# Routing, loading and linear attention in a fused expert-and-attention kernel: three small edits to the order of work

## The chip, the cores and the metric

The kernel runs on one core of a Trainium2 chip. The metric is the device time of one execution in microseconds (us). The core has a matrix engine (TensorE, PE in the profile; its weight loads are PEld), three engines for elementwise work (VectorE or DVE, ScalarE or ACT, GpSimd or POOL), and queues from which DMA transfers are issued (SP's, ScalarE's, GpSimd's). Matrix products go into PSUM banks of 128 x 512 numbers; VectorE and ScalarE read them from there. Each engine works through its own instructions in a fixed order.

## What is computed

All numbers are float32. The input x has shape (4, 512, 256). In short:

```
gate   = rmsnorm(x) @ wg + bias(cond)                 # (4, 512, 8)
w, i   = top 2 of softmax(gate)                       # two of eight experts a token
moe    = sum over the two: w * (relu(relu(x W1 + b1) W2 + b2) W3 + b3)
x      = x + linear_attention(moe)                    # 8 heads, blocks of 32 tokens
x      = x + local_attention_layers(cond_attention(x))  # 16 heads over 512 tokens, then 2 layers
```

In the linear attention each head maps q and k to 128 positive features (elu + 1), and inside a block of 32 tokens

```
num = (qp kp^T masked to the block) v;   z = (qp kp^T masked) 1 + 1e-8;   out = num / z
```

## The kernel before

**Order of work.** Instructions are put on the engines by a list scheduler: it keeps dependencies, takes what is ready in its model in the order of the program, and inserts the waits. `tc.keep_in_program_order(ins)` (used through `pinned(...)` on VectorE and `PE.in_order()` on TensorE) ties an instruction behind the one traced just before it on the same engine. A tile pool hands out `bufs` buffers a tag; a new tile waits until the last reader of the old one is done. `mmt(...)` takes a PSUM bank of the kind "mm" (four in the expert stage and four in linear attention).

**Routing** (L1188 to L1388). TensorE transposes x and forms the gates; four transposes (L1236) bring them back into `pt`. A long chain of small VectorE operations then finds the two best experts of each token (`m`, `eqs`, `rest`, L1254 to L1265), counts with three kinds of products (`ptot` L1286, `ppos` L1288 and L1293, `pcnt` L1292), works out a place for each token, and builds one-hot tiles `ol` and `oh` for the `pmap` products (L1377). `busy(n)` (L1391) issues n products of the identity with xres[0] into a bank that nobody reads; before the change it is defined after the routing and called there with 4, and with 1, 4 and 2 after the experts. `weights()` (L1267) turns the two best gates into the mixing weights `tops`: two subtractions on VectorE, two exponentials on ScalarE, a sum, a reciprocal and a product. In the program it is called at j = 1 of the expert loop (L1495), but the scheduler has moved its work into the routing.

**Experts** (L1488 to L1507). 22 slots of one or two tiles of 128 tokens; each loads its expert's weights on SP, gathers tokens with indirect DMAs, runs three layers with ReLU shared between ScalarE and VectorE (`relu`, L1402 and L1404), and scatters rows to the DRAM tensor `ys`.

**Results** (L1525 to L1544). `results(b)` loads the two expert outputs of batch b from `ys` into tiles g0 and g1 (two buffers each): batch 0 in two halves, k = 0 on SP and k = 1 on ScalarE's queue; every other batch in one load each on SP. `weighted(b, gs)` scales g0 on ScalarE (L1539) and combines on VectorE (L1540) into y[b]. Batches 0 and 1 are loaded at once, then batch 0 is combined; batch 1 is combined in `front(1)`, and `front(b)` loads batch b + 2. `front` also adds a bias to xres[b] on GpSimd (L1561).

**Linear attention** (L1547 to L1700). TensorE's order is written out by hand here. `front(b)` transposes y[b] to yT and forms q, k, v; its copies out of PSUM alternate between ScalarE and VectorE (`evac`, L123 and L125). For each pair of heads `features` forms `pf`, two ScalarE passes `ex` (L1599, L1600) and a VectorE pass `f` (L1602); `scores` forms `psc` and masks it into `sc` (L1612). After each four heads `values(d, g)` forms numerators in the bank `pn` and denominators in the bank `pz`, then

```
nc.scalar.activation(z, pz, AF.Identity, bias=eps8)                              # L1631
nc.vector.reciprocal(z[:, half], z[:, half])                                     # L1636
nc.vector.tensor_tensor(d.aT[:, g, half], pn[:, half], z[:, half], ALU.mult)     # L1637
```

so that `pn` is read last by the product on VectorE. `tail` projects aT and adds to xres. The last batch's pieces run beside `cond_front`, the start of the next attention (`pck`, `pcq`, `fterm` on GpSimd), whose exponentials are `cex` (L420).

Of the kernel before, what the change touches and what calls it, by code (L numbers as in the profile page):

```python
# [15 lines left out]
ALU = mybir.AluOpType  # L16
# [4 lines left out]
NT = S // 128  # L21
# [42 lines left out]
def adaln_attn_ffn_kernel(ctx: ExitStack, tc: tile.TileContext, a: dict, out: bass.AP):  # L64
    nc = tc.nc


    class PE:
        pinned = False
# [36 lines left out]
    def bank(kind, name):  # L106
        return ps_now["pool"].tile([128, 512], F32, tag=kind, name=name, bufs=ps_now[kind])

    def mmt(name):
        return bank("mm", name)  # L110
# [41 lines left out]
    ident = const.tile([128, 128], F32, tag="ident", name="ident")  # L152
    make_identity(nc, ident)
    xres = [const.tile([128, NT, H], F32, tag=f"xres{b}", name=f"xres{b}") for b in range(B)]
# [245 lines left out]
    def cond_stage(W, cp, sp, safe, first=None, v1s=None, before=()):  # L400
# [7 lines left out]
        def attend(fill):  # L408
# [26 lines left out]
            for n in range(len(todo) + 2):  # L435
                if n < len(todo):
                    if n and n % 16 == 0:
                        run(pieces[n // 16 - 1])
                    scores(*todo[n])
                while done:  # L440
                    finish(*done.pop())
                if n < len(todo) and n % 16 != 13:
                    fill(n)
                if 0 < n <= len(todo):
                    values(*todo[n - 1])
# [17 lines left out]
        def attend_safe(d):  # L463
# [39 lines left out]
            for t in range(NT):  # L503
                den = cp.tile([128, CH], F32, tag="cden", name="cden")
                po = None
                for g in range(4):
                    exs = scores(t, g, den)
                    if ahead is not None:
                        values(*ahead)
                    if g == 0:  # L510
                        po = acct("pco")
                    ahead = (t, g, exs, den, po)
            values(*ahead)

        def tail(b, d):
# [628 lines left out]
    with ExitStack() as abc:  # L1144
# [7 lines left out]
        with ExitStack() as moe:  # L1152
# [16 lines left out]
            at, parts = 0, []  # L1169
# [7 lines left out]
            xall = a["x"].rearrange("b s h -> (b s) h")  # L1177

            wgs = xp.tile([128, 2, 32], F32, tag="wgs", name="wgs")
            nc.gpsimd.memset(wgs, 0.0)
# [2 lines left out]
            def pinned(ins):  # L1185
                tc.keep_in_program_order(ins)

            with PE.in_order():  # L1188
# [29 lines left out]
                for c in range(2):  # L1218
                    for b in range(B):
                        PE.matmul(pg[32 * b : 32 * b + 32, :], wgs[:, c, :], xTs[2 * b + c],  # L1220
                                  start=(c == 0), stop=(c == 1))
# [11 lines left out]
            gate = xp.tile(G, F32, tag="gate", name="gate")  # L1233
            pt = tpt("pgt")
            for t in range(NT):
                PE.transpose(pt[:, t * 128 : (t + 1) * 128], gT[:, t * 128 : (t + 1) * 128], ident)  # L1236
            g4 = gate.rearrange("p (b t) e -> p b t e", b=B)
            nc.vector.tensor_tensor(
                g4, pt.rearrange("p (t b e) -> p b t e", b=B, e=32)[:, :, :, 0:NE],
# [6 lines left out]
            def bc(t):  # L1246
                return t.unsqueeze(2).to_broadcast(G)
# [5 lines left out]
            tops = []  # L1253
# [12 lines left out]

            def weights():  # L1267

                nc.vector.tensor_tensor(gate, gate, bc(tops[0]), ALU.subtract)
                nc.scalar.activation(gate, gate, AF.Exp)  # L1270
                nc.vector.tensor_tensor(tops[1], tops[1], tops[0], ALU.subtract)
                nc.scalar.activation(tops[1], tops[1], AF.Exp)
                nc.vector.reduce_sum(tops[0], gate, axis=AX.X)
                nc.vector.reciprocal(tops[0], tops[0])
                nc.vector.tensor_tensor(tops[1], tops[1], tops[0], ALU.mult)
# [15 lines left out]
            pcnt = mmt("pcnt")  # L1291
            PE.matmul(pcnt[:, :NE], tot, mtiles[:, 128:], start=True, stop=True)  # L1292
            PE.matmul(ppos[:, :128], tot, mtiles[:, :128], start=False, stop=True)  # L1293
            E2 = [128, NE, 2 * NE]
            over = xp.tile(E2, F32, tag="over", name="over")
            nc.vector.tensor_tensor(over, pcnt[:, :NE].unsqueeze(2).to_broadcast(E2),
                                    mthr.unsqueeze(1).to_broadcast(E2), ALU.is_gt)

# [60 lines left out]
            for i0 in range(0, B * NT, 4):  # L1359
# [15 lines left out]
                for i in range(i0, i1):  # L1375
                    for k in range(2):
                        PE.matmul(pmap[64 * k : 64 * k + 64, :NHI], ol[:, k, i - i0, :], oh[:, k, i - i0, :],  # L1377
                                  start=(i == 0), stop=(i == B * NT - 1))
# [7 lines left out]
            rowtok = xp.tile([128, NROWT], I32, tag="rowtok", name="rowtok")  # L1386
            nc.vector.tensor_scalar(rowtok, pmap2[:, :NROWT], -1.0, 0.0, ALU.add, ALU.max)
            nc.vector.tensor_single_scalar(rowtok, rowtok, B * S - 1, op=ALU.bitwise_and)  # L1388


            def busy(n):  # L1391
                with PE.in_order():
                    ps = mmt("pbusy")
                    for _ in range(n):
                        PE.matmul(ps, ident, xres[0].rearrange("p t h -> p (t h)")[:, :512], start=True, stop=True)


            busy(4)

            def relu(dst, src, bias):  # L1400
# [87 lines left out]
            for j, d in enumerate(often):  # L1488
                if j == len(often) - 1:
                    aside = conditions(cw_, wp)  # L1490
                    next(aside)
                if j == len(often) - 2:
                    halves = nc.values_load(nhalf[0:1, 0:1], min_val=0, max_val=2 * NE)
                if j == 1:
                    weights()  # L1495
                h1 = layer(d, d.xbT, "h1", d.w1[:, 8:].rearrange("p (c m) -> p c m", m=ME), 0)
                if j:
                    last(j - 1, ds[j - 1])
                if j + 1 < len(often):
                    loads(j + 1, ds[j + 1])  # L1500
                    gather(j + 1, ds[j + 1])
                    if j > 1 and later:
                        name, behind[0] = next(iter(later)), True
                        cw_[name] = later.pop(name)()
                        behind[0] = False
                d.h2 = layer(d, h1, "h2", d.w2, 4)
            last(len(often) - 1, often[-1])  # L1507

            next(aside)
            busy(1)  # L1510
            with tc.If(halves > NHALF - NRARE):
                for j in rare:
                    d = ds[j]
# [4 lines left out]
                    last(j, d)  # L1518
            next(aside)
            busy(4)  # L1520
            run(aside)
            busy(2)


            def results(b):  # L1525
                gs = [gp.tile([128, NT, H], F32, tag=f"g{k}", name=f"g{k}", bufs=2) for k in range(2)]
                n = 2 if b == 0 else NT
                for t in range(0, NT, n):
                    for k in range(2):
                        at = 1 + (k * B + b) * S + t * 128  # L1530
                        queue = nc.scalar if b == 0 and k == 1 else nc.sync
                        queue.dma_start(gs[k][:, t : t + n, :],
                                        ys[at : at + n * 128].rearrange("(t p) h -> p t h", p=128))
                return gs

            def weighted(b, gs):
                for t in range(NT):
                    i = b * NT + t
                    nc.scalar.mul(gs[0][:, t, :], gs[0][:, t, :], tops[0][:, i : i + 1])  # L1539
                    nc.vector.scalar_tensor_tensor(  # L1540
                        y[b][:, t, :], gs[1][:, t, :], tops[1][:, i : i + 1], gs[0][:, t, :], ALU.mult, ALU.add)

            both = {b: results(b) for b in range(2)}
            weighted(0, both[0])  # L1544


        with ExitStack() as lin:  # L1547
# [69 lines left out]
            def values(d, g):  # L1617
                if g == 0:

                    pool, tag = (wp, "aTlast") if d is ds[-1] else (lp, "aT")  # L1620
                    d.aT = pool.tile([128, 2, S], F32, tag=tag, name="aT")
                pn, pz = mmt("pn"), mmt("pz")
                for t in range(NT):
                    for dst in (pn, pz):
                        for i in range(4):
                            h = 4 * g + i
                            lhs = d.v[:, t, 32 * h : 32 * h + 32] if dst is pn else ones32
                            PE.matmul(dst[32 * i : 32 * i + 32, t * 128 : (t + 1) * 128], lhs,
                                      d.scs[h][:, t, :], start=True, stop=True)
                z = lp.tile([128, S], F32, tag="z", name="z", bufs=1)  # L1630
                nc.scalar.activation(z, pz, AF.Identity, bias=eps8)  # L1631

                n = S // 2 if d is ds[-1] and g == 1 else S
                for at in range(0, S, n):
                    half = slice(at, at + n)
                    nc.vector.reciprocal(z[:, half], z[:, half])  # L1636
                    nc.vector.tensor_tensor(d.aT[:, g, half], pn[:, half], z[:, half], ALU.mult)  # L1637

            def tail(b, d):
                for t2 in range(NT // 2):  # L1640
# [30 lines left out]
            with PE.in_order():  # L1671
# [9 lines left out]
                for k in range(len(steps) + 1):  # L1681
                    b, u = steps[k] if k < len(steps) else (B, 0)
# [171 lines left out]
```

## Time and profile before

| | us |
|---|---|
| median of the runs shown (1377.8, 1381.41, 1935.3) | 1381.41 |
| the profiled execution | 1378.49 |
| its span, first to last instruction | 1376.6 |

Busy time of the engines in the stages of the profiled execution (us):

| stage, us from the start | PE | DVE | ACT | POOL | clock granted to PE |
|---|---|---|---|---|---|
| 0 to 20: load, gates | 11.55 | 9.37 | 10.77 | 3.62 | 1.00 |
| 20 to 50: routing, first tokens | 18.32 | 16.05 | 5.89 | 7.71 | 0.77 |
| 200 to 300: experts | 100.00 | 20.64 | 14.93 | 21.54 | 1.00 |
| 300 to 340: results, start of linear attention | 36.62 | 19.36 | 19.29 | 5.41 | 0.96 |
| 340 to 420: linear attention | 75.25 | 57.84 | 47.12 | 0.00 | 1.00 |
| 420 to 500: its end, next attention | 77.28 | 53.61 | 40.21 | 8.37 | 1.00 |

How to read what follows: a row of the timeline gives the start, the time taken, the engine, the line of the kernel, the operation, what it writes and reads, how many instructions are merged, and in brackets how long the engine had been idle and what ended that. A TensorE product in float32 shows as two records. Where several instructions are merged, the time is that from the first start to the last end. A line of a helper (L78 and L82 for products and transposes, L123 and L125 for copies) stands for all its callers, so products are told apart by the tile that they write.

### The profile page before, as it was taken

How to read it: one execution, taken by the hardware profiler on the slowest of the kernel's cores; microseconds unless marked ns; L12 is line 12 of the kernel's file. 1: busy time of each engine (PE TensorE's matmuls, PEld its weight loads, DVE VectorE, ACT ScalarE, POOL GpSimd, SP SyncE). 2: the span in 40 equal slices, each digit the busy share in tenths (PEclk: the TensorE clock that was granted, in tenths of full speed). 3: DMA queues.
4: the chain of work that ended last, by engine and by line, in shares of the span. 5: the costliest groups of instructions: out<-in, count | busy, mean ns of one | idle time of the engine just before them, and what ended most of it. 6: DMA issues, size and time to landing. Idle time of an engine off the chain costs nothing.

```text
span 1376.6 us, 19525 instructions
## 1 busy us (share of the span) xinstructions
PE 1336.3 (97%) x7628; PEld 830.3 (60%) x7628; DVE 653.6 (47%) x1295; ACT 595.8 (43%) x1125; POOL 232.3 (17%) x223
## 2 busy tenths in 40 slices
PE   5999999999999999999999999999999999999998
PEld 4788888884566633433345556656555565556654
DVE  6222121225777743332237697653361777854421
ACT  4111111115555365565656755662222666574111
POOL 1324322211000021010103132000030322310110
PEclk8999999999999999999999999999999999999999
DMA  4577767543000000000220001211001010011000
GB/s 140 208 243 270 238 227 249 192 148 130 1 1 1 1 1 1 1 1 0 89 73 1 18 25 32 86 32 24 24 0 42 24 33 25 17 41 44 20 24 25
DMA packets 43086, 94.74 MB, mean 69 GB/s; under 512 B 9569, under 2 KB 25065, under 8 KB 40169
## 3 DMA queue, kind: packets, MB, share of 16 engines
q1 hardware_dynamic: 37560, 81.81, 18.3%
q0 software_dynamic: 3792, 10.24, 2.3%
q10 hardware_dynamic: 1632, 1.34, 0.3%
q8 instruction: 63, 1.03, 0.3%
q14 instruction: 39, 0.31, 0.1%
HBM read 84.08 MB, written 7.21 MB: 66 GB/s over the span
## 4 chain that ended last, share of the span: by engine, by line
PE 89%; DVE 5%; ACT 2%; DMA 1%; issue 1%; SPq 0%; POOLq 0%; POOL 0%; DVEq 0%
PE ph L78 14%; PE pdq L78 12%; PE pfy L78 6%; PE pug L78 5%; PE sc L78 5%; PE pua L78 5%; PE pv L78 5%; PE po L78 5%; PE pn L78 4%; PE pdy L78 4%; PE pds L78 4%; PE pz L78 2%; PE pqt L82 2%; PE pqk L78 1%; PE pck L78 1%
## 5 line engine op out<-in xcount | busy, mean ns | idle before, releaser
L78 PE MATMUL pdq<-wqkv,yT 128*128 128x512 f32 x384 | 177.1, 603 | 0.2 <-ACT yT L602 0.2
L420 ACT ACTIVATE cex<-sc 128x512 f32<-128x512 f32 x256 | 132.2, 603 | 85.5 <-PE sc L78 85.5
L78 PE MATMUL ph<-h,w 128*128 128x256 f32 (+1 forms) x704 | 132.8, 346 | 1.0 <-issue 1.0
L628 POOL TENSOR_TENSOR qr<-t,t 128x512 f32<-128x512 f32 x64 | 85.9, 1342 | 266.2 <-DVE t L625 225.2
L672 DVE TENSOR_TENSOR p<-p,lmask 128x384 f32<-128x384 f32 (+1 forms) x128 | 92.2, 735 | 69.4 <-ACT p L670 68.2
L78 PEld LDWEIGHTS ph<-h,w 128*128 128x128 f32 x704 | 116.1, 191 | 13.1 <-issue 1.3
L1402 ACT ACTIVATE h<-ph,w 128x256 f32<-128x256 f32 (+1 forms) x88 | 35.4, 438 | 190.7 <-PE ph L78 128.6
L78 PEld LDWEIGHTS pdq<-wqkv,yT 128*128 128x128 f32 x384 | 69.7, 190 | 78.4 <-issue 72.6
L670 ACT ACTIVATE p<-pds,ss 128x256 f32<-128x256 f32 (+1 forms) x256 | 96.1, 457 | 39.1 <-PE pds L78 30.7
L1404 DVE TENSOR_SCALAR h<-ph,w 128x256 f32<-128x256 f32 (+1 forms) x88 | 36.1, 438 | 160.3 <-PE ph L78 102.6
L78 PE MATMUL sc<-qm,kT 32*128 32x512 f32 x512 | 80.6, 639 | 0.0
L78 PE MATMUL pug<-hT,w 128*128 128x512 f32 x160 | 76.8, 602 | 0.0
L618 ACT ACTIVATE sq<-pdq 128x512 f32<-128x512 f32 x64 | 38.3, 598 | 85.4 <-PE pdq L78 47.7
L78 PE MATMUL pua<-hT,w 128*128 128x512 f32 x160 | 75.2, 592 | 0.0
L78 PE MATMUL ph<-xbT,w 128*128 128x256 f32 (+1 forms) x352 | 68.8, 347 | 0.6 <-ACT xbT L123 0.5
L78 PE MATMUL pv<-cex,v 128*32 128x512 f32 x512 | 68.6, 604 | 0.0
L390 POOL TENSOR_SCALAR fterm<-vw,faT 128x256 f32<-128x256 f32 x16 | 14.6, 925 | 316.2 <-DVE cr L380 316.2
L78 PE MATMUL po<-w,h 128*128 128x256 f32 x296 | 67.6, 379 | 0.0
L78 PE MATMUL pds<-qT,kT 64*128 64x256 f32 (+1 forms) x512 | 65.3, 375 | 0.0
L78 PEld LDWEIGHTS pds<-qT,kT 64*128 64x128 f32 x512 | 43.9, 186 | 32.9 <-issue 25.8
L78 PEld LDWEIGHTS ph<-xbT,w 128*128 128x128 f32 x352 | 58.5, 191 | 7.6 <-issue 0.8
L78 PE MATMUL pdy<-wo,oT 128*128 128x256 f32 x256 | 61.5, 386 | 0.0
(301 smaller groups left out, 2130.3 us busy)
## 6 DMA issues: line engine op xcount, KB each, us to landing
w<-in_moe_w_dram SPq DMA_DIRECT2D x22, 1024.0 KB
w<-in_moe_w_dram SPq DMA_DIRECT2D x22, 640.0 KB
w<-in_moe_w_dram SPq DMA_DIRECT2D x22, 516.0 KB
zb<-rows SPq DMA_DIRECT2D x32, 256.0 KB
g<-ys SPq DMA_DIRECT2D x6, 512.0 KB
wqkv<-in_f_wqkv_dram SPq DMA_DIRECT2D x2, 1536.0 KB
w<-in_f_w_dram SPq DMA_DIRECT2D x2, 1408.0 KB
out_dram<-yc SPq DMA_DIRECT2D x16, 128.0 KB
```

Source lines behind the costliest of these rows:

```text
L78: cls._queue(nc.tensor.matmul(*args, **kw))
L82: cls._queue(nc.tensor.transpose(*args, **kw))
L390: nc.gpsimd.tensor_scalar_mul(fterm[:, t, :], vw, W["faT"][:, t, b : b + 1])
L420: nc.scalar.activation(ex[:, i, :], pss[2 * j + i], AF.Exp, scale=CHD**-0.5)
L618: nc.scalar.activation(sq, p3, AF.Square)
L628: nc.gpsimd.tensor_tensor(qr_t[:, s], t1, t2, ALU.add)
L670: nc.scalar.activation(p[:, at], pss[r][:, at], AF.Exp, scale=d.ss[:, 2 * u + jj, 1, 2 * c + r : 2 * c + r + 1])
L672: nc.vector.tensor_tensor(p[:, :n], p[:, :n], lmask[:, :n], ALU.mult)
L1402: nc.scalar.activation(dst, src, AF.Relu, bias=bias)
L1404: nc.vector.tensor_scalar(dst, src, bias, 0.0, ALU.add, ALU.max)
```

## The change

It has three parts.

- *Routing.* `busy` is defined ahead of the routing and called with 4 after the gate transposes and after the second `ppos` product. The two subtractions of `weights()` are pinned behind what is traced before them on VectorE.
- *Results.* Batch 0's tiles 0 and 1 are combined first, then batch 1 is loaded, then batch 0's tiles 2 and 3 are combined. A one-element memset into each of batch 1's tiles, pinned on VectorE, makes the loads wait until VectorE gets there. Batch 1's k = 1 load goes to ScalarE's queue.
- *Linear attention.* ScalarE copies `pn` into aT, and the product on VectorE then works on aT in place.

```diff
@@ routing
+            def busy(n):
+                with PE.in_order():
+                    ps = mmt("pbusy")
+                    for _ in range(n):
+                        PE.matmul(ps, ident, xres[0].rearrange("p t h -> p (t h)")[:, :512], start=True, stop=True)
...
             for t in range(NT):
                 PE.transpose(pt[:, t * 128 : (t + 1) * 128], gT[:, t * 128 : (t + 1) * 128], ident)
+            busy(4)
...
-                nc.vector.tensor_tensor(gate, gate, bc(tops[0]), ALU.subtract)
+                pinned(nc.vector.tensor_tensor(gate, gate, bc(tops[0]), ALU.subtract))
                 nc.scalar.activation(gate, gate, AF.Exp)
-                nc.vector.tensor_tensor(tops[1], tops[1], tops[0], ALU.subtract)
+                pinned(nc.vector.tensor_tensor(tops[1], tops[1], tops[0], ALU.subtract))
...
             PE.matmul(ppos[:, :128], tot, mtiles[:, :128], start=False, stop=True)
+            busy(4)
@@ results
                 gs = [gp.tile([128, NT, H], F32, tag=f"g{k}", name=f"g{k}", bufs=2) for k in range(2)]
+                if b == 1:
+                    for k in range(2):
+                        tc.keep_in_program_order(nc.vector.memset(gs[k][0:1, 0, 0:1], 0.0))
...
-                        queue = nc.scalar if b == 0 and k == 1 else nc.sync
+                        queue = nc.scalar if b < 2 and k == 1 else nc.sync
...
-            both = {b: results(b) for b in range(2)}
-            weighted(0, both[0])
+            both = {0: results(0)}
+            weighted(0, both[0], range(2))
+            both[1] = results(1)
+            weighted(0, both[0], range(2, NT))
@@ linear attention, values(d, g)
                 nc.scalar.activation(z, pz, AF.Identity, bias=eps8)
+                nc.scalar.copy(d.aT[:, g, :], pn)
...
-                    nc.vector.tensor_tensor(d.aT[:, g, half], pn[:, half], z[:, half], ALU.mult)
+                    nc.vector.tensor_tensor(d.aT[:, g, half], d.aT[:, g, half], z[:, half], ALU.mult)
```

More of the change, by code (lines that the diff above doesn't have):

```diff
@@ L1388, in adaln_attn_ffn_kernel @@
             nc.vector.tensor_single_scalar(rowtok, rowtok, B * S - 1, op=ALU.bitwise_and)
[L1391 to L1395, printed above, removed]
             busy(4)
@@ L1534, in results, with weighted @@
                 return gs
-            def weighted(b, gs):
-                for t in range(NT):
+            def weighted(b, gs, at=range(NT)):
+                for t in at:
                     i = b * NT + t
```

## The prediction

> **What bounds the kernel now.** I read the busy table first, then the windows by stage, then the chain of waits, and last the timelines around the three places that the change touches.
>
> ```profile
> span 1376.6 us, 19525 instructions
> PE 1336.3 (97%) x7628; PEld 830.3 (60%) x7628; DVE 653.6 (47%) x1295; ACT 595.8 (43%) x1125; POOL 232.3 (17%) x223
> PE 89%; DVE 5%; ACT 2%; DMA 1%; issue 1%; SPq 0%; POOLq 0%; POOL 0%; DVEq 0%
> ```
>
> TensorE is busy for 97% of the span and carries 89% of the chain that ends last. So at most 1376.6 - 1336.3 = 40.3 us of idle PE can be won, and the change takes no matmul of the computation away (it adds eight). Where is that idle time? The windows put about 20 us into the first 50 us (11.55 busy of 20, 18.32 of 30), and 3.4, 2.6, 2.2 and 2.7 us into 300:340, 340:380, 380:420 and 420:500. Only these stages matter here.
>
> **Part 1, the routing (unread products, pinned subtractions).** The windows of the routing, columns PE, PEld, DVE, ACT, POOL busy, then the granted clock:
>
> ```profile
> 20.00:22.00 2.00, 0.32 (x2) 0.35 (x2) 1.43 (x7) 0.52 (x2) 0.00 (x0) 0.79 0.00 0
> 22.00:24.00 2.00, 1.84 (x8) 1.51 (x7) 1.45 (x8) 0.00 (x0) 0.00 (x0) 0.50 0.00 0
> 24.00:30.00 6.00, 0.00 (x0) 0.00 (x0) 5.62 (x29) 0.47 (x2) 0.00 (x0) 0.50 0.34 89
> 30.00:34.00 4.00, 3.42 (x36) 3.04 (x38) 4.00 (x9) 2.73 (x11) 0.00 (x0) 0.50 1.02 422
> 34.00:36.00 2.00, 1.77 (x30) 1.55 (x29) 1.52 (x3) 1.06 (x4) 0.00 (x0) 0.79 1.05 428
> ```
>
> The clock halves at about 21.2 (0.79 over 2 us is 58% at 1.0, then 0.5), 4.3 us after the gate transposes end at 16.9, and is whole again at about 34.8. In between VectorE is busy and PE is not: the routing is a VectorE chain, and a faster PE helps only where the chain passes through it.
>
> Added: 2 x 4 products. The existing busy(4) at L1398 is eight PE records in 3.70 us. The first new group fits between 16.9 and 20.6, ahead of ptot at 21.68; the second between about 23.3 and 27.0, ahead of the first pmap at 30.36. Their cover is 4.77 and 6.52 us of PE idle; without it each would cost up to 3.70. Both at nothing. What they buy: ptot (two records, 0.56 us) and pcnt (0.55) run at half clock on the chain; pairs as small at full clock (pcs, four outputs) take 0.36 to 0.38. That is 2 x 0.19, so -0.4 us. The pmap products end with 1.02 us for 16 records, already at full clock, and wait for oh and ol on VectorE, so nothing there. Upside down: at full clock pmap fills about half of PE instead of 3.42 of 4 us, and if the clock then falls just before the last 16, they cost 1.0 again instead of being unchanged, +0.6. I take 0.
>
> The pinned subtractions leave the routing chain. The rows show what they cost in it: dependent VectorE operations follow each other every 0.325 us; around the subtraction of L1269 the step is 0.40 (19.55 to 19.95), around L1271 0.32, and the sum, reciprocal and product of L1273 to L1275 lie in the waits for ptot and pcnt or add nothing (23.25 to 23.58). So -0.1 us, not five operations. They move into the expert loop at j = 1, behind the last VectorE instruction of the first slot (52 to 54 us), with 1.14 us on VectorE and, on ScalarE, two exponentials (0.31 + 0.21) and the table load of 1.28 that now lies at 15.54. ScalarE has 2.92 us idle before 56.22 and PE has the last layer of slot 0 to do (po, 1.73 on the chain) ahead of the layer that needs these ReLUs. Taken at 0; if a ReLU queues behind the load, up to 1.8 us once.
>
> [...]
>
> **Part 2, the expert results.** The timeline from the last scatter into linear attention:
>
> ```profile
> 320.64 0.91 ACT L1539 ACTIVATE g<-g,m 128x256 f32<-128x256 f32 x2 [4.72 <-DMA g<-ys]
> 321.95 0.91 ACT L1539 ACTIVATE g<-g,m 128x256 f32<-128x256 f32 x2 [0.41 <-DMA g<-ys]
> 322.06 2.34 POOL L1561 TENSOR_TENSOR xres<-xres,crows 128x1024 f32<-128x1024 f32 x1 [5.20 <-DMA g<-ys]
> 322.49 2.58 DVE L1540 SCALAR_TENSOR_TENSOR ymoe<-g,m,g 128x256 f32<-128x256 f32 x2 [0.35 <-ACT g L1539]
> 324.73 1.73 PE L82 MATMUL pt<-ident,ymoe 128*128 128x128 f32 x6 [2.29 <-DVE ymoe L1540]
> ```
>
> Does the second batch's load slow the first's? Adding up the half-microsecond windows, 0.53 MB had moved by 320.5 and 1.06 MB by 321.9: exactly the first half of batch 0 when its scaling begins, and all of batch 0 when the other half begins. Batch 1 already queues behind on SP. Loading it later gains nothing on arrival. The real stall is another: the third combination should take 0.48 us (median of L1540) and takes 2.18, ending just after POOL's bias addition. That addition starts at 322.06, after the last busy product that reads xres[0] (321.96), and the change moves neither.
>
> Added: two one-element memsets (about 0.1 us each, by the 128x1 memset of 0.10 on POOL) and ScalarE's issue of one load (0.47), which waits for the memsets behind the second combination at about 322.1. Behind it on ScalarE are the scalings of tiles 2 and 3, so these may come 0.9 us later, at 322.9; but VectorE is held until 324.4 anyway, and that is the cover: 0. If the cover were gone, +0.9. Batch 1 lands near 326 instead of 324.6 and is not read by PE before 345.6. Its combinations free the buffers for batch 3, whose scalings sit between feature exponentials on the chain at 333; +0.4 likely hidden, +2 at worst.
>
> **Part 3, the values out of their bank.** Eight ScalarE copies of 128x512 are added, at 0.58 (the yT copy from PSUM), 4.6 us in all; VectorE's product keeps its length (0.67 from PSUM; 0.68 for a 128x512 product of SBUF operands, L1363). The bank comes free after z and the copy, 1.3 us after the products, instead of after a reciprocal of 3.35 and the product, 4.7. Who waits for that bank?
>
> ```profile
> 375.97 1.12 PE L78 MATMUL pqk<-yT,awqkv 128*128 128x512 f32 x2 [0.96 <-DVE aT L1637]
> 376.96 0.68 DVE L125 COPY yT<-pt 128x512 f32<-128x512 f32 x1
> 377.70 1.12 PE L78 MATMUL pqk<-yT,awqkv 128*128 128x512 f32 x2 [0.60 <-DVE yT L125]
> ...
> 446.73 0.58 ACT L293 COPY xT<-pt 128x512 f32<-128x512 f32 x1
> 447.41 1.98 PE L78 MATMUL pck<-xT,cwqkv 128*128 128x512 f32 x4 [1.27 <-DVE aT L1637]
> 449.00 1.22 DVE L1602 SCALAR_TENSOR_TENSOR f<-pf,ex 128x1024 f32<-128x1024 f32 x1
> ```
>
> PE waits 0.96, 0.93 (at 411.52, the same pattern) and 1.27 us for it: 3.2 us. But what is late next? At 375.97 the two records of the first half move up by 0.96, and the second half still waits for the yT copy, which VectorE makes only at 376.96, after reciprocal, product and f. PE then waits 1.56 instead of 0.60 and resumes at 377.70 as before. At 447.41 the product's second half needs the xT copy (447.31), and the next features wait for f, done at 450.2. So the released bank is worth 0; bounds: -3.2 if VectorE's order changes with it. The copies: after z, ScalarE is idle until PE's next result by 0.46 to 2.3 us (waits ahead of L1599), except where a yT or xT copy follows, and there f is late by VectorE, not by ScalarE (about 1 us spare at 375.8). At 482, z ends at 482.69 and the first exponential of the next stage starts at 483.02, so +0.25 of copy beyond the gap, regained before 483.89. I take 0, bound +0.6.
>
> [...]
>
> **Sum.** -0.4 - 0.1 + 0 + 0 = -0.5 us against the profiled execution's 1378.49 (span 1376.6 and 1.9 around it): **1378.0 us**. The expert loop is PE-bound from 48 us on, so what the routing gains goes through. The median of the runs shown is 1381.41 and the lowest 1377.8; a new median may fall anywhere in that spread of 3.6.
>
> **Rivals.**
> - *Nothing on the path* (my forecast), 0.60: 1376.5 to 1382, from -0.9 in copies that fit better to +1.8 for the table load, and the spread of the runs.
> - *The releases reach the path*, 0.20: VectorE's order changes, so the waits on aT and on yT go (3.2 + 2 x 0.6 = 4.4), and the third combination gets ahead of POOL, which saves 2.3 of idle PE and half of the 3.4 us at clock 0.5 after it, 1.7. In full 1378.0 - 8.4 = 1369.6. For it: these are all of the waits that the page names there. Against: each has a second wait behind it.
> - *ScalarE becomes late in linear attention*, 0.20, slower than before: all eight copies stand between z and the feature exponentials, 8 x 0.58 = 4.6, so 1382.6. It decides where ScalarE's idle time ahead of L1599 is under 0.58; the rows have 0.46 to 0.48 in three of eight places and over 2 in others, which speaks against the full price.
>
> The load's deferral doing nothing is part of the forecast already.
>
> **Range and chances.** 1372 to 1385 takes in two thirds of the faster rival, the slower one, and the bounds of +1.8 and +2; the likeliest case's own range is 1376.5 to 1382. A change of 2% is 27.6 us, about what a measurement of this kernel tells from no change; no term comes near it. Faster 0.02, same 0.95, slower 0.03 for a rearranged schedule that I can't see.
>
> **What would show it.** Clock 1.0 in 20:30 and ptot to over shorter by 0.4; L1269 and its table load between 50 and 60; a combination still near 2.2 us beside L1561; no PE wait on aT, but longer ones on yT; PE busy time up by some 7 us. I am wrong if the PE idle of 300:500 falls by over 3 us, or if PE waits for ex or cex grow.

## The result, and the profile after

| | before | after |
|---|---|---|
| median of 20 runs, us | 1381.1 | 1383.22 |
| the profiled execution, its span, us | 1376.6 | 1384.0 |
| TensorE's mean granted clock in it | 0.994 | 0.992 |

The ratio is 1.0018, with a 95% interval of 1.001 to 1.0025: the change costs about 2.5 us (0.0018 x 1381). Forecast were 1378.0 us and a gain of 0.5. The time lies in the range of 1372 to 1385, on the other side of no change. The spans of single executions differ by more than the medians (1376.6 and 1384.0 against medians 2 us apart), so the two profiles are compared stage by stage and not by their ends. One execution of the kernel before, of 1935.3 us, is in its median and not in the ratio.

The page's head, busy table and chain of waits, after:

```profile
span 1384.0 us, 19568 instructions
PE 1348.0 (97%) x7644; PEld 833.9 (60%) x7644; DVE 654.7 (47%) x1297; ACT 599.6 (43%) x1133; POOL 232.8 (17%) x223
PE 89%; DVE 6%; ACT 2%; DMA 1%; issue 1%; another core or an unknown queue 0%; SPq 0%; POOLq 0%; DVEq 0%
```

TensorE is busy for 11.7 us more (forecast: some 7), and still bounds. The timeline shows 3.60 and 5.13 us of that as the two added groups of products.

**Routing.** The same windows as before (PE, PEld, DVE, ACT, POOL busy, granted clock, DMA share, GB/s), then the timelines of TensorE and ScalarE:

```profile
20.00:22.00 2.00, 0.74 (x4) 0.36 (x4) 1.38 (x5) 0.00 (x0) 0.00 (x0) 1.00 0.00 0
22.00:24.00 2.00, 1.94 (x9) 1.24 (x9) 1.40 (x7) 0.00 (x0) 0.00 (x0) 0.69 0.03 8
24.00:30.00 6.00, 4.30 (x9) 1.64 (x8) 5.62 (x27) 0.89 (x4) 0.00 (x0) 0.82 0.40 116
```

```profile
21.66 0.35 PE L78 MATMUL ptot<-ones,pick 128*128 128x1 f32 x2 [1.26 <-DVE pick L1289]
22.40 0.39 PE L78 MATMUL pcnt<-mc,tot 128*128 128x8 f32 x2
...
54.50 1.28 ACT L1278 ACT_TABLE_LOAD   x1
55.80 0.31 ACT L1278 ACTIVATE gate<-gate 128x128 f32<-128x128 f32 x1
```

ptot and pcnt take 0.35 and 0.39 us at full clock (before 0.56 and 0.55), and the first operation behind them, `over`, starts at 22.83 instead of 23.25. From the first VectorE operation behind the gate transposes (17.00, before 16.95) it is 5.83 us, before 6.30. The clock is whole at 20:22 and falls for some 3.4 us at 23 to 27, so the forecast of 1.0 in 20:30 came only in part. The weights' exponentials now lie in the expert loop, and the function follows its table load at once.

**Results.** The start of linear attention:

```profile
323.25 2.34 POOL L1569 TENSOR_TENSOR xres<-xres,crows 128x1024 f32<-128x1024 f32 x1 [5.20 <-DMA g<-ys]
323.65 2.62 DVE L1546 SCALAR_TENSOR_TENSOR ymoe<-g,m,g 128x256 f32<-128x256 f32 x2 [0.38 <-ACT g L1545]
325.93 1.55 PE L82 MATMUL pt<-ident,ymoe 128*128 128x128 f32 x6 [2.37 <-DVE ymoe L1546]
```

The third combination is held beside GpSimd's bias as before (the two take 2.62 us; 2.58 before), and TensorE waits 2.37 us for it (2.29 before). From the transposes of fa to the first q product it is 6.53 us (320.84 to 327.37), before 6.67. Nothing is won or lost.

**Values.** First rows of before: the third front, and the last piece of linear attention beside the next attention:

```profile
371.05 0.69 ACT L1631 ACTIVATE z<-pz,eps 128x512 f32<-128x512 f32 x1 [3.06 <-PE pz L78]
371.77 3.35 DVE L1636 RECIPROCAL z<-z 128x512 f32<-128x512 f32 x1 [1.94 <-ACT z L1631]
373.06 1.95 PE L78 MATMUL psc<-f 128*128 128x128 f32 x16
...
465.03 1.21 DVE L1602 SCALAR_TENSOR_TENSOR f<-pf,ex 128x1024 f32<-128x1024 f32 x1
466.16 0.68 DVE L1647 TENSOR_TENSOR xres<-pao,xres 128x512 f32<-128x512 f32 x1
466.76 1.21 DVE L1602 SCALAR_TENSOR_TENSOR f<-pf,ex 128x1024 f32<-128x1024 f32 x1
467.31 1.89 PE L78 MATMUL pcv<-cwqkv,xT 128*128 128x256 f32 x8
```

After, around the third front, the product at the fourth, and the same last piece:

```profile
371.67 0.40 PE L78 MATMUL pn<-sc,v 128*32 128x128 f32 x8
371.89 0.40 PE L78 MATMUL pz<-sc,ones 128*32 128x128 f32 x8
372.14 0.59 ACT L1641 COPY aT<-pn 128x512 f32<-128x512 f32 x1 [2.84 <-PE pn L78]
372.62 0.69 ACT L1639 ACTIVATE z<-pz,eps 128x512 f32<-128x512 f32 x1
373.35 3.35 DVE L1646 RECIPROCAL z<-z 128x512 f32<-128x512 f32 x1 [2.21 <-ACT z L1639]
374.37 1.95 PE L78 MATMUL psc<-f 128*128 128x128 f32 x16
376.73 0.69 DVE L1647 TENSOR_TENSOR aT<-aT,z 128x512 f32<-128x512 f32 x1
377.34 1.22 DVE L1610 SCALAR_TENSOR_TENSOR f<-pf,ex 128x1024 f32<-128x1024 f32 x1
378.48 0.68 DVE L125 COPY yT<-pt 128x512 f32<-128x512 f32 x1
379.21 1.12 PE L78 MATMUL pqk<-yT,awqkv 128*128 128x512 f32 x2 [2.03 <-DVE yT L125]
...
414.98 1.79 PE L78 MATMUL pqk<-yT,awqkv 128*128 128x512 f32 x2 [2.00 <-DVE yT L125]
...
468.61 2.35 DVE L1610 SCALAR_TENSOR_TENSOR f<-pf,ex 128x1024 f32<-128x1024 f32 x2
470.87 0.68 DVE L1657 TENSOR_TENSOR xres<-pao,xres 128x512 f32<-128x512 f32 x1
471.60 1.99 PE L78 MATMUL pcv<-cwqkv,xT 128*128 128x256 f32 x8 [0.85 <-DVE xres L1657]
```

Three things are to be seen. ScalarE takes the copy *ahead* of z: the last pn product ends before the last pz product, so the copy is ready first, and z, with the whole VectorE row behind it, waits until the copy is through: z starts 1.75 us ahead of the scores' products (`psc`) instead of 2.01. The two waits of before (0.96 and 0.60, with 1.02 us of product between them) have become one of 2.03 us. And where z is later, VectorE makes both f before xres, so the first pcv product waits 0.85 us (no wait there before, where xres lay between the two f).

The windows behind the second long wait (same columns):

```profile
413.00:415.00 2.00, 0.02 (x1) 0.02 (x1) 2.00 (x4) 0.89 (x1) 0.00 (x0) 1.00 0.02 4
415.00:416.00 1.00, 1.00 (x2) 0.27 (x2) 1.00 (x2) 0.00 (x0) 0.00 (x0) 0.65 0.00 0
416.00:417.00 1.00, 1.00 (x5) 0.30 (x8) 1.00 (x3) 0.19 (x1) 0.00 (x0) 0.50 0.00 0
417.00:418.00 1.00, 1.00 (x8) 0.22 (x5) 0.25 (x1) 0.39 (x1) 0.00 (x0) 0.50 0.00 0
418.00:419.00 1.00, 1.00 (x5) 0.28 (x2) 0.00 (x0) 0.18 (x1) 0.00 (x0) 0.64 0.00 0
```

TensorE idles through 413 to 415 and is then busy at half clock for some 3.4 us: the q product of 1.12 us takes 1.79 (row 414.98 above).

A ruler for the rest, read from TensorE's rows (us): the time from the third front's scores to the second half of its first q product, from there to the same product of the fourth front, and on to the first pcv product.

| | before | after | values part, clock whole |
|---|---|---|---|
| scores to q product | 4.64 | 4.84 | 4.84 |
| q product to q product | 35.55 | 35.77 | 35.75 |
| q product to pcv | 54.06 | 56.62 | 54.99 |

The last column is the run below in which products fill the waits, where no half-clock stretch falls into these pieces. So the waits cost 0.20 + 0.20 + 0.93 = 1.3 us, and the other 1.6 us of *after*'s last piece go with the clock.

### The profile page after: what moved, and what is told of

Read it like the earlier page. It is cut to its first block, busy times and chain, and to the rows that moved or that the text cites. A ratio compares the mean times of both kernels' runs of the same rounds, so it can differ in the third digit from the quotient of the medians.

```text
span 1384.0 us, 19568 instructions
## 1 busy us (share of the span) xinstructions
PE 1348.0 (97%) x7644; PEld 833.9 (60%) x7644; DVE 654.7 (47%) x1297; ACT 599.6 (43%) x1133; POOL 232.8 (17%) x223
## 4 chain that ended last, share of the span: by engine, by line
PE 89%; DVE 6%; ACT 2%; DMA 1%; issue 1%; another core or an unknown queue 0%; SPq 0%; POOLq 0%; DVEq 0%
PE ph L78 14%; PE pdq L78 12%; PE pfy L78 6%; PE pug L78 5%; PE sc L78 5%; PE pua L78 5%; PE pv L78 5%; PE po L78 5%; PE pn L78 4%; PE pdy L78 4%; PE pds L78 4%; PE pz L78 2%; PE pqt L82 2%; PE pqk L78 1%; PE pcy L78 1%
```

## The experiments

All ratios are to the kernel before, run beside it on the same chip, with 95% intervals.

**One part at a time, and the change again.** Each is the diff of that part alone.

> Only the routing part of the change. Theory 1 (the loss comes from the released bank in linear attention): -0.4 us or nothing, ratio 0.9997 to 1.0000, VectorE's routing chain 0.4 us shorter as in the changed kernel. Theory 2 (the loss starts in the routing: TensorE reaches the first expert 1.3 us earlier, waits near 45.9 us and drops to half clock behind that wait): about +1.2 us at the first po product (54.0 us before, 55.2 after), ratio about 1.0009, clock near 0.5 between 46 and 50.


Measured 0.9988 (0.9976 to 0.9999). The second theory is out: this part alone is no slower, and no half-clock stretch stands behind 36 us in its profile, but for the last few us (1373 to 1376).

> Only the later load of the second batch. Both theories: the third combination still waits for GpSimd (about 2.2 us, as in both kernels), so 0 +- 0.3 us, ratio 1.0000. If the load counted after all, the transposes of y[0] would start their second run over 0.5 us earlier or later than 7.0 us after the issue of the first load.


Measured 0.9999 (0.9988 to 1.0011).

> Only the copy out of the bank. Theory 1: slower by most of the measured loss, +1.5 to +3 us, ratio 1.0011 to 1.0022; the copy is issued ahead of z, z starts 0.2 to 0.5 us later, and the two idle gaps of TensorE (0.96 and 0.60 before) are one of about 2 us. Theory 2: +0.5 us at most, ratio under 1.0004.


Measured 1.0026 (1.0012 to 1.004). The loss comes with this part. The three parts' times, -1.7, -0.1 and +3.6 us, add up to +1.8, between what the whole change gave (+2.5 above, +1.4 in the next run).

> The changed kernel again, for a second profile: ratio 1.001 to 1.0025 as measured. [...]


Measured 1.001 (1.0 to 1.002). The loss is the values part's; in its trace the rows are those of the change (copy ahead of z, waits of 2.03, 2.00 and 0.85 us). The change's first profile has half-clock stretches at 46 to 50, 415 to 419, 484 to 487 and 716 to 719 us, beside the one at the start of linear attention that both have. Three of these four are gone (46, 415 and 716 us), one stands at the same work (479 to 482), and a new one at 376 to 380: they move from execution to execution.

**What in the values part costs.** Holding the copy behind z, and taking away what is late next:

```diff
-                nc.scalar.copy(d.aT[:, g, :], pn)
+                tc.keep_in_program_order(nc.scalar.copy(d.aT[:, g, :], pn))
```

> The copy out of the bank alone, tied behind z on ScalarE. If the order of copy and z is the cause, the loss goes: z starts as in the kernel before, ratio 1.0000 to 1.0005. If the joined idle gap and the half clock behind it are the cause (the order costs only 0.2 us a place, three places on the path), 0.6 us come back and the ratio stays at 1.0010 to 1.0025, with a gap of about 1.8 us still there in two places.


Measured 0.9989 (0.9979 to 0.9999). One pinned copy turns the loss round. The wait for xres at the first pcv is gone. The two joined waits are not: they are 1.83 and 1.80 us, and the run is no slower than before.

```diff
-                    evac(yT[:, c, :], pt)
+                    nc.scalar.copy(yT[:, c, :], pt)
```

> The copy out of the bank behind z, and both copies to yT on ScalarE, so that the q and k products wait neither for the bank nor for VectorE. If the second wait (for yT on VectorE) is what made the release worthless, the gaps of 0.9 and 0.6 us near 376 and 412 go: 2 to 3 us faster than the same without the yT copies, ratio 0.998 to 1.000. If VectorE's f bounds the stretch anyway, only 0 to 0.5 us, and TensorE waits for f instead.


This with the pin: 1.0004 (0.9994 to 1.0013). The waits of 1.83 and 1.80 us for yT shrink to 0.35, and waits of 1.12 and 1.09 us for f take their place: VectorE's f bounds the stretch.

> Both copies to yT on ScalarE, nothing else changed: the bank is still held until the product on VectorE. The wait for yT (0.6 us, twice) goes and the wait for the bank (0.96 and 0.93) stays: -1.2 us if the bank's wait isn't the whole gap, ratio 0.9991; 0 if VectorE's f bounds the stretch.


This edit alone: 0.9993 (0.9983 to 1.0004); the waits for aT (0.96, 0.93) stay, those for yT become 0.51 for f. The interval holds both values that were expected.

**The third combination.** The unread products read another tile, so that GpSimd's bias no longer waits for them:

```diff
-                        PE.matmul(ps, ident, xres[0].rearrange("p t h -> p (t h)")[:, :512], start=True, stop=True)
+                        PE.matmul(ps, ident, mc[:, :512], start=True, stop=True)
```

> The kernel before with the unread products reading the constants mc instead of xres[0], so that GpSimd's bias addition to xres[0] need not wait for the last of them. If that addition is what holds the third combination, it takes 0.48 us instead of 2.18, TensorE's idle time near 323 falls from 2.3 to about 0.6 us and the half clock behind it (3.4 us) goes: -1.7 to -3.4 us, ratio 0.9975 to 0.9988. If the second half of the data is what comes late, 0.


Measured 0.9998 (0.9987 to 1.001). The timeline of this run at the same place:

```profile
322.79 0.88 DVE L1540 SCALAR_TENSOR_TENSOR ymoe<-g,m,g 128x256 f32<-128x256 f32 x2 [0.30 <-ACT g L1539]
...
325.58 1.30 ACT L1539 ACTIVATE g<-g,m 128x256 f32<-128x256 f32 x3 [2.54 <-DMA g<-ys]
326.79 0.56 ACT L123 COPY yT<-pt 128x512 f32<-128x512 f32 x1
327.40 6.49 PE L78 MATMUL pqk<-yT,awqkv 128*128 128x512 f32 x8 [2.92 <-ACT yT L123]
```

The biases now run at 128 to 137 us, and the two combinations take 0.88 instead of 2.58 us. But ScalarE's yT copy stands behind scalings of the next batch that wait for its load, and TensorE waits 2.92 us for the copy. Of the stall of 2.29 us 0.54 is left, but the clock is low at 326 to 333 us for 6.8 us, twice the 3.4 of before, and the run is no faster.

**Together, and again.**

> The whole change with one thing different: the copy of linear attention's values out of their bank is held behind the bias activation that writes z. Theory A (the copy costs because ScalarE issues it ahead of z, and so reciprocal, product and yT copy on VectorE come later): the parts add up, routing 0.9988 and values with z first 0.9989, so 0.9977 of the kernel before, about 3 us faster, and no wait of the TensorE for xres at the first pcv. Rival B (the order of copy and z is of no weight, the values part differed between two groups of runs for another reason): about 1.0015, as the whole change.


Measured 0.9993 (0.9983 to 1.0003): the change with the one pin. Neither expectation: it beats the change as it stands, but not by the sum of the parts.

> The values part alone, once more, beside the others on one chip. Theory A: 1.0026 again (1.0012 to 1.004). Rival B: nearer to 0.999, where the version with z first lay.


Measured 1.0018 (1.0008 to 1.0028). The loss repeats.

The whole change with z first shows the rows that differ, ScalarE and VectorE:

```profile
368.59 0.69 ACT L1639 ACTIVATE z<-pz,eps 128x512 f32<-128x512 f32 x1 [3.06 <-PE pz L78]
369.17 0.58 ACT L1641 COPY aT<-pn 128x512 f32<-128x512 f32 x1
...
464.95 1.21 DVE L1610 SCALAR_TENSOR_TENSOR f<-pf,ex 128x1024 f32<-128x1024 f32 x1
466.08 0.68 DVE L1657 TENSOR_TENSOR xres<-pao,xres 128x512 f32<-128x512 f32 x1
...
485.51 1.41 POOL L391 TENSOR_TENSOR fterm<-fterm,crows 128x256 f32<-128x256 f32 x2
485.89 1.65 DVE L1647 TENSOR_TENSOR aT<-aT,z 128x256 f32<-128x256 f32 x2
```

z waits for pz and the copy follows; xres is back between the two f. (The last two rows are used further down.)

> The values part alone, with two more products of identity and the first half of yT (they are overwritten by the products that follow in the same bank) ahead of the first q product in the fronts of batches 3 and 4, so that the TensorE works through the two waits of 2.0 us for yT. About 2 x 0.5 us of work in each wait, so the idle stretch falls to about 1.0 us. Theory H (the long idle stretches cost beyond themselves, by the lowered clock after them: 1.6 us at 415 us): 1.0012 to 1.002, and no half-clock stretch at 378 to 381 or 415 to 418 us. Rival L (only the later data cost): 1.0026 as without them.


The edit, in `front`; the added products' results are overwritten:

```diff
                     ps = mmt("pqk")
+                    if b >= 2 and m == 0:
+                        for _ in range(2):
+                            PE.matmul(ps, ident, yT[:, 0, :], start=True, stop=True)
```

Measured 1.0005 (0.9994 to 1.0016). The products took 0.94 us each, not 0.5, so they fill the wait:

```profile
374.24 1.88 PE L78 MATMUL pqk<-yT,ident 128*128 128x512 f32 x4
375.95 1.02 PE L78 MATMUL pqk<-yT,awqkv 128*128 128x512 f32 x2
377.29 1.13 PE L78 MATMUL pqk<-yT,awqkv 128*128 128x512 f32 x2 [0.31 <-DVE yT L125]
```

The q product starts no sooner (4.84 us behind the scores, as without them), but no half-clock stretch follows, at 378 or at 415.

> Routing's part with its two groups of unread products alone; the two subtractions are not held back. Theory P (the products carry the gain of 1.7 us, by the clock of ptot and pcnt and by the wait for the gather that is gone): 0.9988, within 0.0005. Rival S (the subtractions, issued between ptot's copy and the counting, put VectorE's two instructions of some 0.1 to 0.2 us back on the path): 0.9990 to 0.9991, and over about 0.1 to 0.4 us later in the profile than in the routing run.


Measured 0.9993 (0.9982 to 1.0004). From the first VectorE operation behind the gate transposes to `over` it is 5.89 us, in the routing run 5.82: the pinned subtractions are worth 0.07 us of the chain, which the times can't show.

**Filling more waits, and routing a third time.**

> Routing's part alone, once more. Theory P (the TensorE reaches the gathered rows without a wait, and the first expert products with it): 0.9988 to 0.9993. Rival, the sum of the prediction (0.4 us of clock and 0.1 us of VectorE and nothing more): 0.9996.


Measured 1.0002 (0.9991 to 1.0014). With 0.9988 and 0.9993 (the run without the pins) the mean is 0.9994, -0.8 us: the rival's 0.9996 is nearer than the -1.7 of the first run.

```diff
                     pt = mmt("pt")
+                    if not b and not c:
+                        for _ in range(2):
+                            PE.matmul(pt, ident, cw_["aqkv"][:, 0, :512], start=True, stop=True)
```

> Routing's part, and two products of identity and weights (0.94 us each, overwritten by the transposes that follow in the same bank) ahead of the first transposes of linear attention's first front, so that some 1.9 of the 2.3 us are filled in which the TensorE waits there for the third combination. Theory H (idle stretches cost by the clock as well): no half-clock stretch at 323 to 329 us, and 0.6 to 1.5 us faster than routing alone, so about 0.9980 to 0.9985. Rival (the stretch there falls at times of its own, whatever the TensorE does): as the routing run beside it, within 0.0003.


Measured 0.9997 (0.9986 to 1.0008). The stretch at 323 to 329 us is gone, and new waits of 0.33 to 0.87 us for yT, qk and f stand in the 15 us behind it: that piece is not TensorE's alone.

> The whole change with the copy held behind z, and with the added products at linear attention's first, third and fourth front. Theory H with theory A: the lateness of the values part goes with the order (1.4 us to about 0.1), and the stretches at half clock at 323 to 329, 376 to 380 and 412 to 418 us go with the idle time: 0.998 to 0.9985. Rival (the added products only take the place of idle time): 0.9993, as the same kernel without them.


Measured 1.0018 (1.0006 to 1.003).

> The change as it stands, with the added products at linear attention's first, third and fourth front and nothing else. Theory H: of the change's +1.4 to +2.5 us some 2 go (one stretch at 412 to 418 us and one at 323 to 329 us, at 0.6 to 1.6 us each), so about 0.9995; the wait of 0.85 us for xres at the first pcv is still there. Rival (lateness alone costs): 1.0010 to 1.0018, as the change without them.


Measured 1.0036 (1.002 to 1.0051). Both contradict both theories, for a reason that the latter's timeline shows:

```profile
326.76 0.51 ACT L1545 ACTIVATE g<-g,m 128x256 f32<-128x256 f32 x1 [4.62 <-DMA g<-ys]
327.18 0.57 ACT L123 COPY yT<-pt 128x512 f32<-128x512 f32 x1
...
327.79 5.40 PE L78 MATMUL pqk<-yT,awqkv 128*128 128x512 f32 x8 [2.28 <-ACT yT L123]
```

The added products changed the scheduler's order: ScalarE's yT copy again stands behind a scaling that waits for a load. So these two runs can't tell the two theories apart. The next two fill the third and fourth front only, where the orders stay.

> The change as it stands, with the two added products at linear attention's third and fourth front alone. Theory H (the joined waits cost by the clock as well, 1.3 to 1.8 us in the mean, as between the values run and its filled twin): 1.0000 to 1.0006, with no half-clock stretch between 370 and 420 us. Rival L (only the later yT and xres cost): 1.0010 to 1.0018, as without them.


Measured 1.0019 (1.0008 to 1.0029). No stretch between 370 and 420 us, but one at 452 to 456 and one at 483 to 487.

> The whole change with the copy held behind z, and the two added products at the third and fourth front. Theory H with theory A: 0.9985 to 0.9990, the fastest of the versions with the values part. Rival L: 0.9993, as the same kernel without the products.


Measured 1.0 (0.9989 to 1.0011). Theory H is not borne out in this pair: filling gave neither version anything. The order of copy and z gave 0.0019 again.

**Where the half-clock stretches stand.** One profile of each run was kept. Between 370 and 490 us the eight without the values part have two such stretches in all. The four with the copy first and nothing filled have nine; the three with it filled have four; the three with z first (one of them with yT on ScalarE) have four, and the two with z first and filled two. Of the six profiles with waits of 1.8 to 2.2 us at the third or fourth front, five have a stretch right behind one of them; none of the other fourteen has one there.

**The clock, run by run.** Each execution has its span and mean granted clock. Among the executions of the kernel before, the span falls by 0.93 to 1.06 us for each 0.001 of clock (correlation -0.90 to -0.92 in each group): on one chip 16 executions at 0.989 took 1381.5 us in the mean, five at 0.994 took 1376.7. Taking that slope, the difference of the mean spans can be parted. (us against before in the same group; the standard error of the rest is 0.25 to 0.35. That the slope holds for the other kernels is taken, not shown.)

| kernel | difference | by the clock | rest |
|---|---|---|---|
| values | +3.3 | +2.3 | +1.0 |
| values, again | +2.3 | +0.85 | +1.4 |
| values, filled | +1.1 | +0.2 | +0.9 |
| values, z first | -1.0 | +0.35 | -1.4 |
| values, z first, yT copies on ScalarE | +0.4 | +1.4 | -1.0 |
| yT copies on ScalarE | -0.9 | +0.15 | -1.1 |
| unread products from mc | -0.4 | -0.1 | -0.3 |
| results | -0.4 | +0.1 | -0.5 |

The rest of the values part, +1.0 and +1.4, is what the ruler gave for the waits (1.3). Kernels with the routing's products can be compared only with one another, since with those products the clock stays up for longer in the routing, where TensorE has little else to do (half clock for 3.4 us there after, 13.7 before). The change against routing alone: +3.3, of it +2.5 by the clock (0.9938 against 0.9962) and +0.8 rest. The filled pair: 2.2 between copy first and z first at the same clock of 0.9939, so all rest.

## Why the prediction was wrong

**The step that failed** is in part 3: "The bank comes free after z and the copy, 1.3 us after the products", and from it "The copies: after z, ScalarE is idle", taken at 0 with a bound of +0.6. The copies are not after z. ScalarE takes each of the eight ahead of it (the change's profile), so z ends up some 0.25 us later, and the yT copies, f and xres behind the reciprocal with it. Shown by the pin: one instruction's order moves the values part from 1.0026 and 1.0018 to 0.9989, the whole change from 1.0018 and 1.001 to 0.9993, and the filled change from 1.0019 to 1.0. By the ruler the lateness is 1.3 us where 0 stood.

**The term that was left out** is the clock. The forecast had it in the routing and in a rival, and charged no clock to the values part, although its own working said that two waits of 0.96 and 0.60 would become one of 1.56 us. The parting by the clock gives 0.85 to 2.3 us to it; filling the joined waits took the values run from 1.0018 to 1.0005 (the intervals overlap), but the whole change not from 1.0018 or 1.001 (1.0019 filled). The profiles have stretches behind the joined waits and none there without them, so that such a wait can bring one is supported. That it makes the kernel slower is not shown: when the waits are filled, stretches stand at other places, with z first the waits are as joined, with 0.35 us by the clock and no loss, and the run that shortens them to 0.35 us each (yT copies on ScalarE) has 1.4 us by the clock.

**The starting point.** The forecast time began from one execution of 1378.49, 2.6 us under the median of 1381.1. Of the 5.2 us between 1378.0 and 1383.22, 2.6 come from that choice and 2.6 from the change (+2.1 in the medians where -0.5 was forecast).

**What held.** *The released bank is worth 0*, as the change has it: its waits (0.96, 0.93, 1.27) are gone, and TensorE waits for yT, xT and f in their place, at 2.03, 2.00 and 0.35 to 0.60 us. With z first, the order that the forecast supposed, the scores-to-q time is 4.64 us in the trace, exactly that of before. But that run measured 0.9989, -1.5 us and not 0, inside the bound of -3.2. The waits at pck account for 0.3 us (1.27 before, 0.36 and 0.60 now); the remainder is not located. *Results 0*: 0.9999. *Routing -0.4 of clock*: from ptot to `over` it is 1.17 us instead of 1.57, the 0.4 of the forecast, and the subtractions' -0.1 is 0.07 in the rows. The forecast -0.5 lies in the interval of each of the three runs, but so, in two of them, does no gain at all. *The third combination stays*: yes. The second rival's 2.3 us behind it did not come either where the unread products read mc and the combination was no longer held; another order of ScalarE's copy was not tried.

**The rivals.** "ScalarE becomes late in linear attention" had the sign and the engine, but not the mechanism: its condition was a full ScalarE ahead of the exponentials, at 0.58 us a copy, and the first exponential of the third front starts 0.39 us ahead of the scores in both profiles (372.67 to 373.06, 373.98 to 374.37). What came late was z. "The releases reach the path" did not happen.

**The product beside GpSimd.** "VectorE's product keeps its length" was forecast, at 0.67 to 0.68 us. The last one keeps it where GpSimd is done: 0.69 us in the change, from 492.29 us, after GpSimd's additions have ended at 492.14. In the run with z first it meets GpSimd's second addition and takes 1.65 us, ending 0.6 us after it. Before, with `pn` read from PSUM, it took 0.69 us beside the same addition. VectorE's wait for its next work shrinks from 2.23 to 0.92 us, so the longer product cost nothing.

## What to carry to other kernels

An instruction added next to a critical one under a list scheduler can be issued ahead of it, whatever its place in the text: read which operand ends first, and pin the order if it matters. When a released wait is "taken over by the next", look at whether two short idle pieces become one long one: half-clock stretches stood behind five such waits here, though their price was not settled. And before a stall is attacked, read what its engines queue behind it: the stall of 2.29 us was cut to 0.54 here, and a copy behind a waiting load took its place.

## What the runs showed of the hardware

Stretches at a granted clock of 0.50, some 3.4 us long, appear behind waits of 2.0 to 2.2 us (2.00 at 415 us in the change's profile, 2.03 at 375 in its second, 2.17 at 411 in the run with z first), and at 476 to 487 us where TensorE waits only 0.42 and 0.41 us between small products. The same kernel has them in some executions and not in others: of the change's two profiles one has a stretch at 415 to 419 us, the other at 376 to 380. The profiles have none to five of them between 300 and 500 us, and a product under one takes up to 1.8 times as long (2.07 us for pvw in the run of the results part, 1.13 before). In a program whose TensorE is busy for 97%, the mean clock goes with some four fifths of the variance of its executions (correlation -0.9), whose spans lie between 1376.6 and 1382.6 us on one chip.
